# One issue order for a whole four-layer graph kernel, constants loaded on demand, a split layer norm, and an attention product built from rows times Wv·Wo

## The chip, the cores and the metric

The kernel runs on one core of a Trainium2 chip, in float32. A core has a matrix engine (TensorE, "PE" in the profile, with its weight loads shown apart as "PEld"), VectorE ("DVE"), ScalarE ("ACT"), GpSimd ("POOL") and SyncE ("SP", which here only issues transfers). Each engine works through its own list of instructions in order; between engines there are only semaphores. A transfer (DMA) is issued from an engine's queue, and an issue that must wait holds up what is behind it on that queue. Matrix products go to PSUM, of which there are 8 banks of 128 partitions by 512 float32.

The metric is the device time of one execution in microseconds (us).

## The reference

128 graphs of 64 nodes with 256 features, 8192 rows in all, go through four layers. Each layer computes `x = x + layer(relu(layernorm(x)))`:

```
# layer 0: two graph convolutions, then LSTMs over windows of 1, 2, 3 and 4 nodes
h = relu(adj @ (h @ Wg0 + bg0));  h = relu(adj @ (h @ Wg1 + bg1))
for p in 1..4:                       # LSTM p has its own weights
    wins = windows of p consecutive nodes of h
    h[last node of every window] = last hidden state of LSTM_p(wins)
# layer 1: normalised adjacency, two products, batch norm over all 8192 rows after each
h = relu(batchnorm((A_hat @ x) @ W1.T + b1));  out = batchnorm(h @ W2.T + b2)
# layer 2: diagonal, upper and lower part of adj, each with its own W
out = adj_0 @ (x @ W[0]) + adj_1 @ (x @ W[1]) + adj_2 @ (x @ W[2]) + bias
# layer 3: causal attention inside each graph, one head
q, k, v = split(x @ Wqkv);  y = softmax(q k^T / 16 + mask) @ v;  out = y @ Wo
```

The two batch norms need statistics over all rows, so nothing after them can begin for any row before all rows have passed.

## The kernel before, in words

The rows are cut into 16 blocks `s` of 512 rows (8 graphs), each 4 times 128 rows. Every stage runs over these blocks.

**Start (L86 to L118).** The identity and small constants are made, and thirteen loads of constants and first weights are issued from ScalarE's queue: the two adjacencies, bg0, Wg0, Wg1, bg1, the LSTM's and the batch norms' parameters, and W1 (L316, whose issue stands with them since a scheduler orders the work outside the hand-ordered parts). The blocks of x are loaded from SP's queue.

**Stage 1, `graph_part` (L265).** Five steps per block: layer norm and relu (`layernorm_relu`, L168: statistics on VectorE, the power −0.5 on GpSimd, the row scale and shift back on VectorE at L180, and four activations on ScalarE at L183), an aggregation over the adjacency (L193), the product with Wg0 (L289), a second aggregation, and the product with Wg1 (L300). `pipelined` (L220) issues in every round one step of each living block, the newest block first; a new block begins every `skew` rounds. The result `hT` stays in SBUF, features on partitions.

**Stage 2, the LSTMs (L357 to L556).** The order is written out by hand: `at(t, fn)` notes an action with a due time `t` in units of one gate product (a pair of a Wih and a Whh product, two instructions each of 512 columns), and the actions are issued in order of their due times. The gate products follow a Strassen-Winograd scheme with seven products in place of eight. `gate` (L417) has products on TensorE (L430, L436), copies out of PSUM on ScalarE and VectorE (L455), sums on VectorE (L452) and the activations on ScalarE (L448).

**Stage 3, `first_product` (L329).** Per block: x is loaded again on SP and the LSTM result copied on GpSimd (step 1); it is transposed back to rows and x added, the sum stored to DRAM (x1d), and the layer norm issued (step 2, L203, L183); it is aggregated with the normalised adjacency (step 3); multiplied by W1 (L348, step 4); and its batch-norm statistics are taken (step 5, L353). The first three blocks begin inside the LSTM's last step: `begin` and the `times` at L572 give the due times of their steps. The other 13 blocks follow with `pipelined`.

**Between (L582).** `bn_coeffs` turns the statistics of all four channel groups into scale and shift: aggregation, add, power on GpSimd, and three small operations.

**Stage 4, `second_product` (L629).** Eight pairs of blocks, again with due times: relu with scale and shift on ScalarE (L639), four sums T1 to T4 for each half k of the inner dimension (k=0 on VectorE, k=1 on GpSimd, L647 to L653), seven products (L663, each of two halves k), then sums and statistics. After it the weight products: Wq·Wk^T and Wv·Wo (L723, from transposes of Wqkv, L717).

**Stage 5, `rest` (L731).** Layers 2 and 3 per block, in ten steps with skew 2: load of x1d and scaling of y; transposes to rows, add, layer norm; three aggregations (L755); the product with the three W (L768), add, layer norm; transposes (L779); the qk product (L786, `h·Wq·Wk^T`); scores and softmax (L794 to L804); transposes of the exponentials (eT, L808); eT times h (yT, L816, copied out on ScalarE); and yT times Wv·Wo (L824), scaled by the softmax sums, added and stored. The order outside these hand-ordered parts (the constants' loads, `bn_coeffs`, the late weights) is left to a scheduler.

Of the kernel before, what the change touches and what calls it, by code (L numbers as in the profile page):

```python
# [9 lines left out]
F32 = mybir.dt.float32  # L10
AF = mybir.ActivationFunctionType
ALU = mybir.AluOpType
# [8 lines left out]
def kernel(ctx: ExitStack, tc: tile.TileContext, a: dict, out: bass.AP):  # L21
# [28 lines left out]

    const = ctx.enter_context(tc.tile_pool(name="const", bufs=1))
# [20 lines left out]
    def load_const(name, src, shape, pool=const):  # L72
        t = pool.tile(shape, F32, tag=name, name=name)
        nc.scalar.dma_start(t, src)
        return t

    def row_bcast(name, src, n, pool=const):
        t = pool.tile([P, n], F32, tag=name, name=name)
        nc.scalar.dma_start(t, bass.AP(tensor=src.tensor, offset=src.offset, ap=[[0, P], [1, n]]))
        return t  # L80

    def weight(name, src, pool=const):
        k, m = src.shape
        return load_const(name, src.rearrange("(c p) m -> p c m", p=P), [P, k // P, m], pool)
# [17 lines left out]
    bg0 = row_bcast("bg0", a["bg0"], D, first)  # L102
    wg0 = weight("wg0", a["Wg0"], first)
    wg1 = weight("wg1", a["Wg1"], first)
    bg1 = load_const("bg1", a["bg1"], [P, KC], first)
    bih = load_const("bih", a["bih"], [P, NL, NM])
    bhh = load_const("bhh", a["bhh"], [P, NL, NM])
    bn1 = load_const("bn1", a["bn1"], [P, 3, HC])
    bn2 = load_const("bn2", a["bn2"], [P, 3, KC])
# [18 lines left out]
    def adjacencies():  # L128

        nc.vector.tensor_add(lbias, bih, bhh)  # L130
# [37 lines left out]
    def layernorm_relu(pool, src, tag="ln_h", bufs=None, h=None):  # L168
# [4 lines left out]
        if h is None:  # L173
            h = pool.tile([P, Q, D], F32, tag=tag, name=tag, bufs=bufs)
        for q in range(Q):
# [5 lines left out]
                                       op0=ALU.mult, op1=ALU.mult)  # L181
        for q in range(Q):
            nc.scalar.activation(h[:, q, :], src[:, q, :], AF.Relu,  # L183
                                 bias=rn[:, 1, q : q + 1], scale=rn[:, 0, q : q + 1])
        return h
# [34 lines left out]
    def pipelined(gens, skew, live=()):  # L220

        gens, live, r = list(gens), list(live), 0
        with tc.manual_schedule():
            while gens or live:
                if gens and r % skew == 0:
                    live.insert(0, gens.pop(0))
                live = [g for g in live if next(g, "end") != "end"]
                r += 1  # L230
# [32 lines left out]
    with tc.tile_pool(name="pa", bufs=2) as pa, tc.tile_pool(name="pax", bufs=3) as pax:  # L263

        def graph_part(s):  # L265
# [3 lines left out]
            for q in range(Q if s == 0 else 1):  # L269
                part = slice(q, q + 1 if s == 0 else Q)  # L270
                nc.sync.dma_start(xt[:, part, :], x_r[s, :, part, :])
            h = layernorm_relu(pa, xt)
# [24 lines left out]
            for o in range(KC):  # L297
                p_ = bank()
                for c in range(KC):
                    nc.tensor.matmul(p_, wg1[:, c, ts(o, P)], g1[:, c, :],  # L300
# [3 lines left out]
                    t.rearrange("p (q n) -> p q n", q=Q), bcast_q(rs_row), bg1[:, o : o + 1],  # L304
# [11 lines left out]
    w1 = weight("w1", a["W1T"])  # L316
    pb, front = [], ExitStack()
# [11 lines left out]
    def first_product(s):  # L329
# [11 lines left out]
        h = layernorm_relu(lns, xt, h=hs.rearrange("p (q d) -> p q d", q=Q))  # L341
# [3 lines left out]
        for o in range(HC):  # L345
            p_ = bank()
            for c in range(KC):
                nc.tensor.matmul(p_, w1[:, c, ts(o, P)], ag[:, c, :],  # L348
                                 start=(c == 0), stop=(c == KC - 1))
            nc.scalar.activation(zslot(s, o), p_, AF.Identity, bias=bn1[:, 0, o : o + 1])  # L350
        yield
        for o in range(HC):
            nc.vector.bn_stats(st1[:, o, s, :], zslot(s, o))  # L353
        yield
# [204 lines left out]
    early = [None] * 3  # L559
# [12 lines left out]
    for s, times in enumerate(((10.5, 12.5, 25.5), (11.5, 28.5, 33), (13, 36))):  # L572
# [3 lines left out]
    with tc.manual_schedule():  # L576
        for _, _, fn, args in sorted(events, key=lambda e: e[:2]):
            fn(*args)
# [3 lines left out]
    def bn_coeffs(pool, stats, nch, prm, name):  # L582
# [289 lines left out]
```

## Time and profile before

| | us |
|---|---|
| median of 3 runs (1935.64 to 1936.22) | 1936.01 |
| the profiled execution's own time | 1937.42 |
| its span in the profile | 1935.7 |
| TensorE busy (98% of the span, 7060 matrix instructions) | 1890.1 |
| VectorE busy (57%) | 1099.9 |
| ScalarE busy (44%) | 852.1 |
| GpSimd busy (29%) | 557.4 |
| mean granted TensorE clock | 0.994 of full |

How to read the rows of the profile: in the list of waits, a row names the waiting engine, what it wrote and at which line, then what released it, and then the total time, the number of times and the longest, all in us. In a timeline a row has the start, the duration (of several alike instructions in a row, where `xN` stands at the end), engine, line, operation, output and inputs, sizes, and in brackets the idle time before it with what ended it. An engine with a `q` after its name is its instruction queue (issues of transfers). In the table by windows a row has the stretch and its length, then the busy time of TensorE, its weight loads, VectorE, ScalarE and GpSimd with the number of instructions, then the granted TensorE clock as a share of full speed, the share of the DMA engines and GB/s. In the chain a row has its start, its duration, engine and line, and the number of instructions. An x column of numbers like `128x512` gives partitions by elements.

### The profile page before, as it was taken

To read this page: it belongs to the slowest core of one execution; us is meant where nothing else is said; L and a number is where in the kernel's file an instruction comes from. 1 tells how busy PE (TensorE), PEld (TensorE's weight loads), DVE (VectorE), ACT (ScalarE), POOL (GpSimd) and SP (SyncE) were. 2 spreads that over 40 slices of the span, in tenths; PEclk is the share of its full clock that TensorE was granted. 3 is DMA by queue.
4 is the path that set the end of the run, shared out by engine and by line. 5 is a ranking of instruction groups with operands and counts; after the bars stand their busy time and mean duration, and the time that the engine had idled before them with its cause. 6 is when DMAs were issued, how large, how long until landed. Compare 5 with 4: busy or idle time off the path is not lost.

```text
span 1935.7 us, 19149 instructions
## 1 busy us (share of the span) xinstructions
PE 1890.1 (98%) x7060; PEld 1152.6 (60%) x7060; DVE 1099.9 (57%) x2132; ACT 852.1 (44%) x1430; POOL 557.4 (29%) x366
## 2 busy tenths in 40 slices
PE   7999999999999999999999999999899899999998
PEld 6776444444445666665444444555444688888887
DVE  6775777634546345445533334588686555556553
ACT  3554666534435335334433333344574343333332
POOL 1210322443325433232422224433153211111110
PEclk9999999999999999999999999999999999999999
DMA  5110000100001000000000001233100101111111
GB/s 157 55 34 1 1 1 13 31 0 0 0 0 44 1 1 1 1 1 22 0 0 1 1 0 55 88 109 109 41 0 22 33 11 34 44 44 45 44 34 44
DMA packets 49469, 54.29 MB, mean 28 GB/s; under 512 B 3040, under 2 KB 44768, under 8 KB 49376
## 3 DMA queue, kind: packets, MB, share of 16 engines
q1 hardware_dynamic: 45872, 49.81, 8.1%
q10 hardware_dynamic: 3504, 3.26, 0.5%
q8 instruction: 56, 0.92, 0.2%
q14 instruction: 37, 0.30, 0.1%
HBM read 36.28 MB, written 16.78 MB: 27 GB/s over the span
## 4 chain that ended last, share of the span: by engine, by line
PE 93%; DVE 2%; issue 2%; ACT 1%; POOL 1%; DMA 1%; DVEq 0%; POOLq 0%; ACTq 0%
PE ps L430 33%; PE ps L436 19%; PE ps L768 9%; PE ps L663 5%; PE ps L348 5%; PE ps L193 5%; PE ps L824 3%; PE ps L289 3%; PE ps L300 3%; PE ps L786 2%; PE ps L755 2%; PE ps L816 1%; PE ps L794 1%; PE ps L203 1%; PE ps L779 1%
## 5 line engine op out<-in xcount | busy, mean ns | idle before, releaser
L452 DVE TENSOR_TENSOR gate<-gate,ps 128x512 f32<-128x512 f32 (+2 forms) x378 | 223.7, 619 | 457.2 <-PE ps L436 377.7
L430 PE MATMUL ps<-tx,wih 128*128 128x512 f32 (+2 forms) x1008 | 449.4, 545 | 6.0 <-ACT gate L455 4.0
L430 PE MATMUL ps<-hT,wih 128*128 128x512 f32 (+2 forms) x756 | 338.5, 541 | 0.0
L430 PEld LDWEIGHTS ps<-tx,wih 128*128 128x128 f32 x1008 | 191.3, 191 | 196.9 <-issue 133.7
L455 ACT COPY gate<-ps 128x512 f32<-128x512 f32 (+2 forms) x252 | 134.5, 534 | 379.2 <-PE ps L436 325.5
L448 ACT ACTIVATE gate<-gate,lbias 128x512 f32<-128x512 f32 (+2 forms) x252 | 216.7, 860 | 153.9 <-DVE gate L452 153.9
L436 PE MATMUL ps<-h,whh 128*128 128x512 f32 (+2 forms) x576 | 257.5, 529 | 0.0
L430 PEld LDWEIGHTS ps<-hT,wih 128*128 128x128 f32 x756 | 143.7, 190 | 142.4 <-issue 80.2
L179 POOL TENSOR_TENSOR ln_rn<-ln_rn,mhalf 128x4 f32<-128x4 f32 x64 | 64.8, 1012 | 520.9 <-DVE ln_rn L178 520.9
L436 PE MATMUL ps<-th,whh 128*128 128x512 f32 (+2 forms) x432 | 193.4, 529 | 0.0
L436 PEld LDWEIGHTS ps<-h,whh 128*128 128x128 f32 x576 | 109.7, 191 | 100.8 <-issue 77.1
L768 PE MATMUL ps<-wl,ag 128*128 128x256 f32 x768 | 168.4, 379 | 0.0
L475 POOL TENSOR_TENSOR gate<-gate 128x1024 f32<-128x1024 f32 (+2 forms) x36 | 71.9, 2018 | 310.9 <-ACT gate L448 310.9
L768 PEld LDWEIGHTS ps<-wl,ag 128*128 128x128 f32 x768 | 144.7, 190 | 19.0
L183 ACT ACTIVATE ln_h<-x,ln_rn 128x256 f32<-128x256 f32 x128 | 66.4, 589 | 189.3 <-DVE ln_rn L180 189.3
L475 POOL TENSOR_TENSOR cell<-gate 128x1024 f32<-128x1024 f32 (+2 forms) x36 | 79.4, 2226 | 200.1 <-ACT gate L448 200.1
L436 PEld LDWEIGHTS ps<-th,whh 128*128 128x128 f32 x432 | 82.7, 191 | 76.3 <-issue 58.5
L348 PE MATMUL ps<-ag,w 128*128 128x512 f32 x256 | 112.3, 592 | 0.0
L475 POOL TENSOR_TENSOR cell<-gate,cell 128x1024 f32<-128x1024 f32 (+2 forms) x32 | 65.1, 2053 | 103.6 <-ACT gate L448 103.6
L455 DVE COPY gate<-ps 128x512 f32<-128x512 f32 (+2 forms) x126 | 78.6, 624 | 22.6 <-PE ps L436 22.6
L448 ACT ACTIVATE gate<-ps,lbias 128x512 f32<-128x512 f32 (+2 forms) x126 | 79.6, 632 | 4.0 <-PE ps L436 1.0
L480 ACT ACTIVATE gate<-cell 128x1024 f32<-128x1024 f32 (+2 forms) x72 | 68.1, 952 | 27.9 <-POOL cell L475 27.9
(187 smaller groups left out, 2587.6 us busy)
## 6 DMA issues: line engine op xcount, KB each, us to landing
xt<-in_x_dram SPq DMA_DIRECT2D x31, 512.0 KB, 4.4
x1d<-xt SPq DMA_DIRECT2D x16, 512.0 KB, 3.0
x<-x1d SPq DMA_DIRECT2D x16, 512.0 KB, 4.5
out_dram<-x SPq DMA_DIRECT2D x16, 512.0 KB, 3.2
wih<-in_WihT_dram SPq DMA_DIRECT2D x16, 256.0 KB, 4.9
whh<-in_WhhT_dram SPq DMA_DIRECT2D x12, 256.0 KB, 5.0
wqkv<-in_Wqkv_dram ACTq DMA_DIRECT2D x1, 768.0 KB, 4.3
wl<-in_W_dram ACTq DMA_DIRECT2D x3, 256.0 KB, 3.1
```

Source lines behind the costliest of these rows:

```text
L183: nc.scalar.activation(h[:, q, :], src[:, q, :], AF.Relu, bias=rn[:, 1, q : q + 1], scale=rn[:, 0, q : q + 1])
L193: nc.tensor.matmul(p_[:, ts(q, P)], h[:, q, ts(c, P)], mT, start=True, stop=True)
L348: nc.tensor.matmul(p_, w1[:, c, ts(o, P)], ag[:, c, :], start=(c == 0), stop=(c == KC - 1))
L430: nc.tensor.matmul(wide(p_[:, :N]), wih[0][:, OF[k], gi, :], x_, start=first_, stop=(j == 0), skip_group_check=True)
L436: nc.tensor.matmul(p_[:, :N], whh[0][:, OF[k], gi, :], h_, start=False, stop=True, skip_group_check=True)
L448: nc.scalar.activation(to, r[bank_][:, :N] if bank_ else to, fn, bias=lbias[:, l, m : m + 1])
L452: nc.vector.tensor_add(slot(n, hc), slot(n, hc), r[bank_][:, :N])
L455: op(slot(n, hc), r[bank_][:, :N])
L475: fn(*((t["G"] if isinstance(t, dict) and "G" in t else st["c"])[:, n, :, : st["N"]] for t in tiles))
L480: nc.scalar.activation(o_, c, AF.Tanh)
L663: nc.tensor.matmul(banks[name], w2[:, OF[j], k, :], x_, start=(new and k == 0), stop=(k == 1), skip_group_check=True)
L768: nc.tensor.matmul(p_[:, q, :], ag[:, c, k, ts(q2 + q, P)], wl2[k][:, c, :], start=(n == 0), stop=(n == 3 * KC - 1))
```

## The change

All of the kernel is now issued in the order in which it is written; no part is left to a scheduler.

- **Constants on demand.** ScalarE's queue keeps the two adjacencies, bg0 and Wg0. Wg1, bg1, the LSTM biases, the batch-norm parameters and W1 are loaded from SP's queue, in front of block 3's x. A small Relu activation (`warm`) stands on ScalarE behind the loads. The late weights (the three W, bias, Wqkv, Wo) go to SP's queue too, behind the last store of stage 3.
- **Layer norm in two parts.** `layernorm_relu` becomes `norm_of` (statistics and row scale) and `normalize_relu` (the four activations). In `first_product`, for blocks 0 to 2, there is a step between the two, and the due times are new.
- **Batch-norm coefficients by halves.** In the last block, `bn_coeffs` is called after every second channel group.
- **First pair of the second product.** Of the eight relus two run on VectorE (two operations each), the sums of k=1 run on VectorE in place of GpSimd, and the first two products are issued as halves k=0, k=1. The order of the first relus changes.
- **Wv·Wo** is formed after block 0's transposes in `rest`.
- **Attention.** In place of `(eT·h)·(Wv·Wo)`, `hw = h·(Wv·Wo)` is formed beside qk, in the same step, and the output is `eT·hw`. One step per block goes away; `ln_h3` has two buffers in place of four.

```diff
+    ctx.enter_context(tc.manual_schedule())
...
-    wg1 = weight("wg1", a["Wg1"], first)
...
+    bg0 = row_bcast("bg0", a["bg0"], D, first, nc.scalar)
+    wg0 = weight("wg0", a["Wg0"], first, nc.scalar)
+    warm = const.tile([P, 1], F32, tag="warm", name="warm")
+    nc.scalar.activation(warm, mhalf[:, 0:1], AF.Relu)
+    con = {}
+
+    def more_constants():
+        con["wg1"] = weight("wg1", a["Wg1"], first)
+        con["bg1"] = load_const("bg1", a["bg1"], [P, KC], first)
+        con["bih"] = load_const("bih", a["bih"], [P, NL, NM])
+        con["bhh"] = load_const("bhh", a["bhh"], [P, NL, NM])
+        con["bn1"] = load_const("bn1", a["bn1"], [P, 3, HC])
+        con["bn2"] = load_const("bn2", a["bn2"], [P, 3, KC])
+        con["w1"] = weight("w1", a["W1T"])
...
+            if s == 2:
+                more_constants()
             h = layernorm_relu(pa, xt)
...
-        h = layernorm_relu(lns, xt, h=hs.rearrange("p (q d) -> p q d", q=Q))
+        rn = norm_of(lns, xt)
+        if s < len(early):
+            yield
+        h = hs.rearrange("p (q d) -> p q d", q=Q)
+        normalize_relu(h, xt, rn)
...
         for o in range(HC):
             nc.vector.bn_stats(st1[:, o, s, :], zslot(s, o))
+            if s == NS - 1 and o % 2:
+                bn_coeffs(lns, co1, st1, o - 1, o + 1, con["bn1"], "bn1")
...
-    for s, times in enumerate(((10.5, 12.5, 25.5), (11.5, 28.5, 33), (13, 36))):
+    for s, times in enumerate(((10.5, 12.5, 16.5, 28.3), (11.5, 22.3, 26.2, 31), (13, 33, 36.5))):
...
             def relu(n, c):
-                nc.scalar.activation(z(n, c), z(n, c), AF.Relu, bias=co1[:, 1, c : c + 1],
-                                     scale=co1[:, 0, c : c + 1])
+                if i == 0 and n == 1 and c % 2 == 0:
+                    nc.vector.tensor_scalar(z(n, c), z(n, c), co1[:, 0, c : c + 1],
+                                            co1[:, 1, c : c + 1], op0=ALU.mult, op1=ALU.add)
+                    nc.vector.tensor_scalar_max(z(n, c), z(n, c), 0.0)
...
-            for k, (n, c) in enumerate(((0, 1), (0, 3), (0, 0), (0, 2), (1, 0), (1, 2), (1, 1), (1, 3))):
+            for k, (n, c) in enumerate(((0, 1), (0, 0), (0, 3), (0, 2), (1, 0), (1, 2), (1, 1), (1, 3))):
                 at((-6.3, -5.8, -5.3, -4.4, -3.9, -3.4, -2.4, -1.9)[k], relu, n, c)
-            for k, engine in enumerate((nc.vector, nc.gpsimd)):
+            for k, engine in enumerate((nc.vector, nc.gpsimd if i else nc.vector)):
...
-                at(t, product, name, j)
-            at(2, lambda: evict(y(0, 0), 0, "a"))
+                if i == 0 and t < 2:
+                    at(t, product, name, j, (0,))
+                    at(t + 1.1, product, name, j, (1,))
+                else:
+                    at(t, product, name, j)
+            at(2.2, lambda: evict(y(0, 0), 0, "a"))
...
             to_token_major(lambda c, q: y[c][:, ts(q, P)], x1, x2)
+            if s == 0:
+                weight_product(2, wo, wvo)
...
-            h = layernorm_relu(pc, x3, "ln_h3", 4)
+            h = layernorm_relu(pc, x3, "ln_h3")
...
                 nc.scalar.copy(qk[:, o, :], p_)
+            hw = pc.tile([P, Q, D], F32, tag="hw", name="hw")
+            for q2 in range(0, Q, 2):
+                p_ = bank().rearrange("p (q d) -> p q d", q=2)
+                for q in range(2):
+                    for c in range(KC):
+                        nc.tensor.matmul(p_[:, q, :], h3T[:, c, ts(q2 + q, P)], wvo[:, c, :],
+                                         start=(c == 0), stop=(c == KC - 1))
+                nc.scalar.copy(hw[:, q2 : q2 + 2, :], p_)
...
-            yT = pc1.tile([P, KC, SUP], F32, tag="yT", name="yT")
-            for c in range(KC):
-                p_ = bank()
-                for q in range(Q):
-                    nc.tensor.matmul(p_[:, ts(q, P)], h[:, q, ts(c, P)], eT[:, ts(q, P)],
-                                     start=True, stop=True)
-                nc.scalar.copy(yT[:, c, :], p_)
             yield
             for q2 in range(0, Q, 2):
                 p_ = bank().rearrange("p (q d) -> p q d", q=2)
                 for q in range(2):
-                    for c in range(KC):
-                        nc.tensor.matmul(p_[:, q, :], yT[:, c, ts(q2 + q, P)], wvo[:, c, :],
-                                         start=(c == 0), stop=(c == KC - 1))
+                    nc.tensor.matmul(p_[:, q, :], eT[:, ts(q2 + q, P)], hw[:, q2 + q, :],
+                                     start=True, stop=True)
```

The rest of the diff puts `bn_coeffs` on a range of channel groups with a given output tile, gives the load helpers a queue argument (SP where none is named), wraps a weight product into the function `weight_product`, and moves the reciprocal of the softmax sums behind the copy of eT.

## The prediction

> **What bounds the kernel now.** I read the page first (busy shares, the 40 slices, the chain by engine), then the waits of TensorE, then the timeline round every wait over 1 us. The page:
>
> ```profile
> PE 1890.1 (98%) x7060; PEld 1152.6 (60%) x7060; DVE 1099.9 (57%) x2132; ACT 852.1 (44%) x1430; POOL 557.4 (29%) x366
> ...
> PE   7999999999999999999999999999899899999998
> ...
> PE 93%; DVE 2%; issue 2%; ACT 1%; POOL 1%; DMA 1%; DVEq 0%; POOLq 0%; ACTq 0%
> ```
>
> TensorE is 98% busy and 93% of the chain; four slices of 40 fall below 9. To be won is TensorE work that goes away, or time in which it stands or runs slowly. Where it stands (total us, times, longest):
>
> ```profile
> PE ps L193 <- ACT ln_h L183: 8.2, 1, 8.2
> ...
> PE ps L755 <- ACT ln_h L183: 5.2, 1, 5.2
> PE ps L663 <- ACT hS L639: 4.9, 1, 4.9
> PE ps L430 <- ACT gate L455: 4.0, 3, 3.0
> PE ps L193 <- ACT hs L183: 3.9, 1, 3.9
> ...
> PE ps L755 <- ACT qk L788: 1.6, 2, 1.0
> ```
>
> All are at seams between stages. TensorE's timeline puts them in place:
>
> ```profile
> 14.95 6.70 PE L193 MATMUL ps<-adjT_bd,ln_h 128*128 128x128 f32 x32 [8.18 <-ACT ln_h L183]
> ...
> 1202.39 2.08 PE L430 MATMUL ps<-tx,wih 128*128 128x512 f32 x2 [2.96 <-ACT gate L455]
> ...
> 1236.37 3.98 PE L193 MATMUL ps<-ahT,hs 128*128 128x128 f32 x16 [3.95 <-ACT hs L183]
> ...
> 1395.32 2.07 PE L663 MATMUL ps<-hS,w 128*128 128x512 f32 x2 [4.86 <-ACT hS L639]
> ...
> 1505.73 4.45 PE L755 MATMUL ps<-adj,ln_h 64*128 64x192 f32 x32 [5.20 <-ACT ln_h L183]
> ```
>
> After each wait the matmuls are slow: 16 aggregation matmuls take 3.98 us here and 1.95 at 1222.73, a pair 2.08 instead of 1.02. The windows give the granted clock (third column from the end): 0.50 after the wait, 1.00 again some 7 us later. A wait so costs itself and about 3 us more.
>
> ```profile
> 1202.00:1203.00 1.00, 0.61 (x1) 0.50 (x2) 0.00 (x0) 1.00 (x2) 0.00 (x0) 0.50 0.01 3
> 1209.00:1210.00 1.00, 1.00 (x4) 0.52 (x3) 0.69 (x1) 0.00 (x0) 0.00 (x0) 1.00 0.00 0
> ```
>
> **The change part by part**, against the profiled execution (1937.42 us, span 1935.7), which lies 1.41 above the median of 1936.01.
>
> *Start.* ScalarE's queue issues 13 loads before its first activation; the row scale of block 0 is ready long before:
>
> ```profile
> 8.38 0.16 DVE L180 SCALAR_TENSOR_TENSOR ln_rn<-ln_mv,ln_rn 128x4 f32<-128x4 f32 x1 [1.21 <-POOL ln_rn L179]
> ...
> 13.00 1.28 ACT L183 ACT_TABLE_LOAD   x1 [13.00 <-DMA wih<-in_WihT_dram]
> ```
>
> Six loads of constants and W1's leave this queue, and the table load follows the wg0 issue (this and wg1's end at 6.55): it ends by 7.8, and block 0 is normalised from 8.6 (first quarter 0.6) instead of 14.3. The first aggregation starts at 9.2, not 14.95, a gain of 5.7 for block 0. Block 1's row scale still comes at 13.57, so its aggregation waits to 14.2, and TensorE, idle between, stays at half clock. By then block 0's Wg0 product has moved ahead of block 2's aggregation: with block 1's aggregation (32 half-clock matmuls took 6.5, so 3.3) to 17.5 and the product (3.5 at full clock, more where cold), block 2's aggregation starts at about 22.0 where it was 24.94. I take 3.0; bounds 0 (all eaten by the cold clock) and 5.7. The seven loads go to SP in front of block 3's x: it was issued at 16.40, waiting for its buffer, which now comes free near 11; the seven issues cost 0.45 each (the last W1 issue took 0.45) and land within 5.2, so by 16 to 17, against a need near 22. Cover 5 us. One layer's Wih, loaded at 9.06 before, is now loaded after stage 1, some 60 us ahead of its weight sums. Both cost nothing.
>
> *Stage 1 and the LSTM.* Every engine's instructions stand in the same order as before until the last LSTM step: no change, the gain at the start is carried through.
>
> *The LSTM's end.* ScalarE stood 10.05 us behind the row scale (L180, ready at 1199.7) of the normalise it had been given too early, so the gate copy L455 came late, and TensorE waited for its bank. At 1236.37 block 1's aggregation waited in the same way. Now the row scale is asked for one event earlier than the normalise: block 0's transposes at 12.5 and its normalise at 16.5, 4 units of 1.715 us (two pairs of 0.86) = 6.9 us, where the chain from transposes to scale took 1193.25 to 1199.7 = 6.5; block 1 has 3.9 units (6.7 us) and its aggregation 8.2 us later, for four activations of 2.08. Removed: standing 1199.28 to 1202.39 (3.1) and 1232.26 to 1236.37 (4.1); slow clock 1202.39 to 1209.00 = 6.61 for work of 3.43 (3.2), and 1236.37 to 1243.16 = 6.79 for 3.51 (3.3). Sum 13.7. What comes late next: a bank freed by VectorE 0.9 us before it is needed, one by ScalarE 1.0 us, block 3's copies on POOL 1.4 us, block 3's x (on SP behind block 2's store and four W2 loads) 1.6 us, by adding the rows' durations in the new order. If one fails, TensorE stands a little; if by 3 us, it also goes slow. Bounds 8 and 13.7.
>
> *First to second product.* The coefficients are now made in two halves: those of channels 0 and 1 hang on the second statistics (1388.5) and come at about 1391.5; those of 2 and 3 (eight small operations and POOL's 1.01) at 1395.8, where all came at 1394.42. The first two half products (k=0) start at 1392.4, not 1395.32, then k=1 waits to about 1396.6: idle of 1.9 and 2.6 instead of 4.86. VectorE gets two relus (two operations each, about 0.5) and POOL's four sums for pair 0; the eight sums take 0.69 each alone (0.69 at 1398.12; 1.16 to 1.76 where POOL worked beside it), 1397.8 to 1403.3, no later than before. The sixth product then ends at 1401.9 if the clock stays, 1404.3 if not; before at 1404.66. I take 1.2; bounds 0 and 2.7. The six late loads go from ScalarE to SP behind the last store, a hundred us before their use at 1494: nothing.
>
> *Second product to the rest.* The Wv·Wo product (1.73) moves behind block 0's transposes, into the idle 5.20: transposes start at 1498.9 (scaled y is ready then) instead of 1499.49, so the wait ends 0.6 earlier, and 3.5 idle are left. If that idle no longer cools the clock, 4.45 falls to 2.87, 1.6 more. I take 1.0; bounds 0.5 and 2.3.
>
> *The rest.* Per round the chain has these, of 25.96 us:
>
> ```profile
> 1599.06 1.79 PE ps L816 x16
> ...
> 1615.95 3.46 PE ps L824 x16
> ```
>
> They become 16 matmuls of 256 columns (hw, 3.46) and 8 (out, 1.73): 0.06 a round, 1.0 in 16. ScalarE copies two hw banks instead of two yT banks, the same 0.57 each; the reciprocal stays on VectorE beside TensorE's work, and fewer ln_h3 buffers suffice since `h` is read only by the transposes: nothing. In the first rounds hw fills the place where L755 waited for the qk copies (1546.33 to 1547.35, 1545.69 to 1546.15, 1568.21 to 1569.37: 2.6). I take 2.6; bounds 1 and 3.1 (all of the waits there). In steady rounds the nearest copy is 0.9 us ahead of its need. The tail only sees work that was done earlier: 0.
>
> Sum: 3.0 + 13.7 + 1.2 + 1.0 + 1.0 + 2.6 = 22.5. 1937.42 − 22.5 = 1914.9 for a profiled execution, 1913.5 as a median. All lower ends: 0+8+0+0.5+0+1 = 9.5, so 1926.5; all upper ends: 5.7+13.7+2.7+2.3+1.0+3.1 = 28.5, so 1907.5.
>
> A rule weighed: the trace cooled the clock in a wait of 2.96 us at 1202.39 and did not in one of 3.22 us at 1527.6 (transposes there 0.175 each, 1.40 for eight). [...]
>
> **Rivals.**
> - *The cover at the LSTM's end is too thin.* One of the four slacks of 0.9 to 1.6 us fails and a wait of about 3 us with a slow clock comes back: 6.3 less, 1919.8. For: SP's queue is longer there. Against: four separate slacks must each be misjudged by their whole size.
> - *The clock eats the start.* TensorE stays at half clock until after block 2's aggregation as before: 3.0 less, and with both gaps cold at the second product (0.8 less) 1917.3. For: half clock until 21.4 before. Against: block 0's product comes earlier by order alone.
> - *Slower: ScalarE falls behind in the rest.* Its queue now has qk's two copies, hw's two copies and the exps closer together; if hw's banks come free late, every round waits. 22.5 + 3.9 is reached at 1.65 us a round of 16, that is copies 2.5 us later than by the 0.9 of slack; price at that point 1940. For: L755 waited 1.0 for the qk copies in two early rounds. Against: ScalarE is 44% busy and in the steady rounds waited for nothing.
> - *It does not do what it says.* If the LSTM's end kept its waits, 13.7 less: 1927.2. Against: the events are spelled out, and the new order has the split.
>
> **How the numbers follow.** About 0.2% (3.9 us) tells from no change here. Forecast 0.66, thin cover 0.13, clock 0.13, ScalarE behind 0.04, no effect 0.04. Faster by over 0.2%: 0.94; within: 0.02; slower: 0.04. The range takes in the first two rivals and most of the bounds: 1907 to 1924.
>
> **What would show it.** First aggregation at about 9.2 and the LSTM's first matmul some 3 us earlier; no wait over 1 us and no 0.50 clock between 1190 and 1245; block 0's W1 product starting about 13.7 + 3.0 earlier than 1244.03; two short waits in place of 4.86 at the second product; L755's wait near 3.5; rounds of 25.9. It is wrong if the LSTM's end has a wait over 2 us, if a round exceeds 26.2, or if TensorE waits for a load.

## The result, and the profile after

The changed kernel takes 1918.22 us in the median of four runs (1916.92 to 1918.94) where the kernel before took 1935.83 beside it: 17.6 us less, a ratio of 0.9909 (95% interval 0.9892 to 0.9926). The forecast was 1913.5 with a range of 1907 to 1924. The direction and the range hold; the time is 4.7 us above the forecast, and 4.9 us of the 22.5 are missing. Run a second time beside the last experiments, it took 1917.25 (1916.66 to 1918.94) against 1936.04.

The profiled execution has a span of 1917.0 us against 1935.7, so 18.7 less. TensorE is busy 1884.5 us. First the waits of TensorE in the changed kernel (total us, times, longest):

```profile
PE ps L207 <- ACT ln_h L191: 6.7, 2, 3.7
PE ps L132 <- DMA adjT_bd<-in_adjT_dram: 4.2, 1, 4.2
PE ps L783 <- ACT ln_h L191: 3.5, 1, 3.5
PE ps L807 <- DVE ag L788: 3.2, 1, 3.2
PE ps L684 <- ACT z L660: 1.6, 1, 1.6
PE ps L684 <- ACT hS L660: 1.5, 1, 1.5
...
PE ps L684 <- ACT hS L688: 1.1, 1, 1.1
...
PE ps L217 <- DVE hS L762: 0.9, 1, 0.9
PE ps L851 <- DVE eT L845: 0.8, 1, 0.8
```

Both waits at the LSTM's end are gone, and so are the qk copies. The wait before the second product (4.9) is now two of 1.5 and 1.6, and a third of 1.1 follows among its first products, for the copy at L688 out of a bank, which the prediction did not list. The wait that stood before the rest is 3.5 instead of 5.2. Two more lines are new: the transposes at L217 wait 0.9 for the scaled y, and the last product 0.8 for the copy of eT. L807 waits 3.2 as before.

TensorE's timeline of the changed kernel at the places of the prediction:

```profile
8.02 3.70 PE L207 MATMUL ps<-adjT_bd,ln_h 128*128 128x128 f32 x16 [3.03 <-ACT ln_h L191]
15.38 3.98 PE L207 MATMUL ps<-adjT_bd,ln_h 128*128 128x128 f32 x16 [3.67 <-ACT ln_h L191]
...
23.79 1.95 PE L207 MATMUL ps<-adjT_bd,ln_h 128*128 128x128 f32 x16
...
1229.04 7.03 PE L365 MATMUL ps<-ag,w 128*128 128x512 f32 x16
...
1376.95 1.98 PE L684 MATMUL ps<-hS,w 128*128 128x512 f32 x4 [1.48 <-ACT hS L660]
1380.58 1.98 PE L684 MATMUL ps<-z,w 128*128 128x512 f32 x4 [1.65 <-ACT z L660]
...
1487.87 4.99 PE L783 MATMUL ps<-adj,ln_h 64*128 64x192 f32 x32 [3.47 <-ACT ln_h L191]
...
1510.27 1.97 PE L807 MATMUL ps<-ident,ln_h 128*128 128x128 f32 x8 [3.22 <-DVE ag L788]
...
1908.72 3.45 PE L851 MATMUL ps<-hw,eT 128*128 128x256 f32 x8 [0.78 <-DVE eT L845]
```

Compared with the rows of before: block 0's first aggregation starts at 8.02 instead of 14.95, but block 1's only at 15.38. Block 0's W1 product starts at 1229.04 instead of 1244.03. The four matmuls at 1376.95 take 1.98, full speed (the same took 2.07 for two before). L783 takes 4.99 for what is 2.87 at full speed, L807 1.97 where before it took 1.40, and the last L851 3.45 where the others take 1.89. Windows of the changed kernel show why, by the granted clock (third column from the end):

```profile
1490.00:1491.00 1.00, 1.00 (x10) 1.00 (x8) 0.56 (x1) 0.48 (x1) 1.00 (x1) 0.50 0.00 0
...
1511.00:1512.00 1.00, 1.00 (x6) 1.00 (x6) 1.00 (x3) 1.00 (x4) 0.00 (x0) 0.50 0.00 0
...
1910.00:1911.00 1.00, 1.00 (x4) 0.82 (x3) 0.50 (x2) 0.00 (x0) 0.00 (x0) 0.50 0.00 0
```

TensorE is at work there, at half clock (0.50). A ledger by stage, from the starts of the same instructions in both traces (the stretch before minus the stretch after):

| stretch | before | after | gained | forecast |
|---|---|---|---|---|
| start to block 0's transposes in the LSTM | 1193.25 | 1191.94 | 1.3 | 3.0 |
| to block 0's W1 product | 50.78 | 37.10 | 13.7 | 13.7 |
| to the first transpose of Wqkv | 250.00 | 247.43 | 2.6 | 1.2 |
| to the first product with the three W | 17.01 | 17.25 | −0.2 | 1.0 |
| to the second such product | 18.66 | 19.73 | −1.1 | 0 |
| to the end | 406.00 | 403.55 | 2.4 | 3.6 |
| span | 1935.7 | 1917.0 | 18.7 | 22.5 |

So 13.7 of 18.7 us come from the LSTM's end, exactly as worked out; the shortfall stands at the start, at the seam before the rest, and in the rest. The experiments ask for each why.

### The profile page after: what moved, and what is told of

Read it like the earlier page. It is cut to its first block, busy times and chain, and to the rows that moved or that the text cites. A ratio compares the mean times of both kernels' runs of the same rounds, so it can differ in the third digit from the quotient of the medians.

```text
span 1917.0 us, 18932 instructions
## 1 busy us (share of the span) xinstructions
PE 1884.5 (98%) x6932; PEld 1148.2 (60%) x6932; DVE 1098.9 (57%) x2144; ACT 849.0 (44%) x1429; POOL 552.0 (29%) x363
## 4 chain that ended last, share of the span: by engine, by line
PE 95%; DVE 2%; POOL 1%; ACT 1%; issue 1%; DMA 0%; ACTq 0%; DVEq 0%; POOLq 0%
PE ps L449 33%; PE ps L455 19%; PE ps L796 9%; PE ps L365 6%; PE ps L684 5%; PE ps L207 4%; PE ps L303 3%; PE ps L822 3%; PE ps L314 3%; PE ps L814 3%; PE ps L783 2%; PE ps L830 1%; PE ps L217 1%; PE ps L851 1%; PE ps L807 1%
```

## The experiments

Unless said otherwise each edit is to the changed kernel. Stretches and starts are from the profiled execution of each; medians are of four runs. The runs were made in sets, and the kernel before ran beside each: it took 1935.83 beside the changed kernel, 1936.62 beside bg0 first, the LSTM's end alone, all undone before the second product and the attention product as before, 1937.42 beside the two fillings and the two halves of the second product's seam, and 1936.04 beside the last three. So medians of different sets can be compared to about 1.5 us, no closer.

**bg0 first.** In the changed kernel VectorE waits 2.98 us for bg0 at the row sums:

```profile
10.52 0.35 DVE L130 TENSOR_SCALAR rsb<-bg,rs_col 128x256 f32<-128x256 f32 x1 [2.98 <-DMA bg<-in_bg_dram]
```

The load was issued at 0.81 before, first on its queue though written behind the adjacencies, and is issued at 3.63 now, in the order as written; it lands after 6.8 us instead of 4.1. Block 1's statistics stand behind it in VectorE's order.

```diff
+    bg0 = row_bcast("bg0", a["bg0"], D, first, nc.scalar)
     adjT_bd = block_diag("adjT_bd", a["adjT"])
     adj_bd = block_diag("adj_bd", a["adj"])
-    bg0 = row_bcast("bg0", a["bg0"], D, first, nc.scalar)
```

> The changed kernel, with the load of bg0 issued first on ScalarE's queue instead of behind the four adjacency loads. Theory A (bg0 is what VectorE waits for: in the changed kernel it stands 2.98 us at the row-sum product until bg0 lands at 10.5, and block 1's layer norm is queued behind it): that wait goes, block 1's row scale comes at 12 to 13.4 instead of 14.7, its aggregation starts at 12.7 to 14.1 instead of 15.38, and everything after is 1.0 to 2.7 us earlier: 1915.5 to 1917.2 against 1918.2. Theory B (the half clock of the first matmuls sets the start, not the load): block 2's aggregation stays within 0.5 us of 23.79, the time within 0.5 of 1918.2.

Measured: 1914.43 (1913.51 to 1916.91). The timeline of this kernel, VectorE and TensorE:

```profile
8.95 0.35 DVE L130 TENSOR_SCALAR rsb<-bg,rs_col 128x256 f32<-128x256 f32 x1
...
12.96 0.16 DVE L185 SCALAR_TENSOR_TENSOR ln_rn<-ln_mv,ln_rn 128x4 f32<-128x4 f32 x1 [1.12 <-POOL ln_rn L184]
```
```profile
13.81 3.87 PE L207 MATMUL ps<-adjT_bd,ln_h 128*128 128x128 f32 x16 [0.94 <-ACT ln_h L191]
...
20.97 1.95 PE L207 MATMUL ps<-adjT_bd,ln_h 128*128 128x128 f32 x16
```

The wait for bg0 is gone and block 1's row scale comes 1.6 us earlier than in the changed kernel (13.12 against 14.69). Block 2's aggregation starts at 20.97 instead of 23.79, block 0's transposes in the LSTM at 1189.11. Theory A holds for the wait and for block 1; the median lies below its range, and not all of the 2.8 belongs to bg0: eight profiled executions with the start of the changed kernel have these transposes at 1189.7 to 1191.9, mean 1190.4. The two executions with only bg0 moved at the start have 1189.1 and 1189.6 (the second is the last kernel below), so bg0 first brings 0.8 to 1.3, and the start as changed has gained 2.8 (1.3 in the worst, which is the one profiled first).

The rest of the 2.8 is the clock. The trace's own record of the granted clock has no entry for the first microseconds; the views show 1.00 there, while the matmuls run at half rate (block 1's 16 take 3.87 to 3.98 us in the five executions below, block 2's 1.95 at full clock). The last entry of the start is the one from which the clock is full until the later seams:

| execution | block 1's aggregation starts | clock full from | block 2's aggregation starts |
|---|---|---|---|
| changed kernel | 15.38 | 21.53 | 23.79 |
| changed kernel again | 15.14 | 19.65 | 22.73 |
| filled waits | 14.33 | 20.58 | 22.79 |
| halves undone | 14.24 | 18.05 | 21.49 |
| bg0 first | 13.81 | 17.44 | 20.97 |

In each of the five, block 2's aggregation starts 5.34 us (within 0.01) behind the mean of the two times before it, as it must if the work between runs at half rate until the clock is full (the changed kernel's clock was full from 11.29 to 14.70 too, while TensorE mostly stood). So in these five half of every delay, of block 1 or of the clock, arrives at block 2. Of the 2.8 between the changed kernel and bg0 first, block 1's earlier start makes 0.8 and the clock's earlier rise 2.0. The filled waits and the halves undone have the same edits at the start and block 1 within 0.1; the clock parts them by 1.3. Three further executions fit the relation within 0.02; the run with all undone and the one with the VectorE work undone (both below) had full clock until 16 us and come 0.1 to 0.2 earlier than by it.

**The LSTM's end alone**, put into the kernel before: the split of the layer norm and the due times, nothing else.

```diff
-        h = layernorm_relu(lns, xt, h=hs.rearrange("p (q d) -> p q d", q=Q))
+        rn = norm_of(lns, xt)
+        if s < 3:
+            yield
+        h = hs.rearrange("p (q d) -> p q d", q=Q)
+        normalize_relu(h, xt, rn)
...
-    for s, times in enumerate(((10.5, 12.5, 25.5), (11.5, 28.5, 33), (13, 36))):
+    for s, times in enumerate(((10.5, 12.5, 16.5, 28.3), (11.5, 22.3, 26.2, 31), (13, 33, 36.5))):
```

> The kernel before, with only the layer norm of blocks 0 to 2 split and the new due times at the LSTM's end. Theory A (each part acts on its own seam and the gains add): 13.7 us less than before, 1922.1 from 1935.8, with block 0's W1 product at 1230.3 instead of 1244.03 and no wait over 1 us between 1190 and 1245. Theory B (the LSTM's end also needs the other order of loads: late weights on SP, W1 early): less than 11 us, with a wait left at the LSTM's end.

Measured: 1927.0 (1926.65 to 1927.17), 9.6 us less than the kernel before. Theory A gave 13.7, theory B less than 11 with a wait left; neither is right. The timeline of TensorE in this kernel:

```profile
1229.99 2.31 PE L358 MATMUL ps<-ag,w 128*128 128x512 f32 x5
...
1492.48 4.95 PE L765 MATMUL ps<-adj,ln_h 64*128 64x192 f32 x32 [5.20 <-ACT ln_h L184]
...
1514.84 1.97 PE L789 MATMUL ps<-ident,ln_h 128*128 128x128 f32 x8 [3.22 <-DVE ag L770]
1516.60 1.91 PE L209 MATMUL ps<-ident,hS 128*128 128x128 f32 x8
1518.31 11.68 PE L778 MATMUL ps<-wl,ag 128*128 128x256 f32 x48
```

The stretch to the W1 product is 37.10 where it was 50.78: the whole 13.7, with no wait left. The rest of it is given back where nothing was edited. The wait of 3.22 at 1511.6 is the one that the kernel before has too; there the transposes behind it took 1.40 and 1.04, here 1.97 and 1.91, and the product behind them 11.68 instead of 10.53. In all: 0.8 more up to the transposes of Wqkv, 0.5 at L765, 1.4 and 1.2 behind L789, together 3.8 of 13.7 + 0.4. The same waits cost more, because the clock falls or stays by the moment at which a wait begins (behind the one of 3.22 it is 0.50 from 1513.82 to 1520.65 here, and 1.00 throughout in the kernel before). What that moment counts against is shown below.

**The seam before the second product as before** (coefficients at once, all relus on ScalarE, the k=1 sums on GpSimd, whole products, and the old order of the first relus), and then each half of this undone alone. The coefficients come after all four statistics here, so the wait is 6.1, not 4.9.

```diff
-            if s == NS - 1 and o % 2:
-                bn_coeffs(lns, co1, st1, o - 1, o + 1, con["bn1"], "bn1")
+        if s == NS - 1:
+            bn_coeffs(lns, co1, st1, 0, HC, con["bn1"], "bn1")
...
-                if i == 0 and n == 1 and c % 2 == 0:
+                if False:
...
-            for k, engine in enumerate((nc.vector, nc.gpsimd if i else nc.vector)):
+            for k, engine in enumerate((nc.vector, nc.gpsimd)):
...
-                if i == 0 and t < 2:
+                if False:
```

> The changed kernel, with the seam between first and second product as before: all coefficients at once, all relus on ScalarE, the k=1 sums of pair 0 on GpSimd, the first products whole. Theory A (the two short waits keep the clock at full, where one wait of 4.9 us halves it): 2.6 us slower than the changed kernel, 1920.8, a wait of about 4.9 us and the granted clock at 0.50 after it. [...]

The halves undone, the work left on VectorE (the first and last hunk above, and the old order of the first relus):

> The changed kernel with the coefficients made at once and the first products whole again, but with two relus and all sums of pair 0 still on VectorE. Theory A (splitting the one long wait in two is what keeps the clock at full): 3 us slower than the changed kernel in the stretch from block 0's W1 product to the end of the second product, with a wait of 5 to 6 us and 0.50 clock. Theory B (the work on VectorE brings it): less than 1 us slower there.

The halves kept, the work put back on ScalarE and GpSimd (the two middle hunks):

> The changed kernel with the halves kept, but all relus of pair 0 on ScalarE and its k=1 sums on GpSimd. Theory A (the halves alone bring the gain): within 1 us of the changed kernel in the stretch from block 0's W1 product to the end of the second product, no 0.50 clock there. Theory B: 1.5 to 3 us slower there, since the relus come late and sums on GpSimd and VectorE slow each other (1.16 to 1.76 us a sum against 0.69).

| | halves | VectorE work | W1 product to transposes of Wqkv | 0.50 clock there | median |
|---|---|---|---|---|---|
| all undone | no | no | 251.30 | 6.8 us | 1921.49 |
| halves undone | no | yes | 250.77 | 6.8 us | 1918.84 |
| VectorE work undone | yes | no | 248.84 | none | 1916.92 |
| changed kernel | yes | yes | 247.43 | none | 1918.22, 1917.25 |

The wait that decides, in the kernel with all undone, and in the one with halves (VectorE work undone):

```profile
PE ps L684 <- ACT hS L660: 6.1, 1, 6.1
```
```profile
PE ps L684 <- ACT z L660: 1.7, 1, 1.7
PE ps L684 <- ACT hS L688: 1.6, 1, 1.6
PE ps L684 <- ACT hS L660: 1.5, 1, 1.5
```

In the stretch itself theory A holds for the halves: they bring 2.5 to 3.3 us, the VectorE work 0.5 to 1.4. With all undone the stretch is 3.9 longer where theory A gave 2.6, as the wait is 6.1; with the VectorE work undone it is 1.4 longer, outside theory A's 1 us and short of theory B's 1.5. All four executions with one long wait here (4.85 to 6.1, before and the LSTM's end alone among them) lose the clock, none of the nine with short waits does. The medians do not show it cleanly: the kernel with the VectorE work undone has the lower median although its stretch is 1.4 longer.

**The attention product as before**, with yT and one step more:

```diff
-            hw = pc.tile([P, Q, D], F32, tag="hw", name="hw")
-            ...
+            yT = pc1.tile([P, KC, SUP], F32, tag="yT", name="yT")
+            ...
-                    nc.tensor.matmul(p_[:, q, :], eT[:, ts(q2 + q, P)], hw[:, q2 + q, :],
-                                     start=True, stop=True)
+                    for c in range(KC):
+                        nc.tensor.matmul(p_[:, q, :], yT[:, c, ts(q2 + q, P)], wvo[:, c, :],
+                                         start=(c == 0), stop=(c == KC - 1))
```

> The changed kernel, with the attention product as before: yT from eT and h, then yT times Wv Wo, one step more per block, four ln_h3 buffers. Theory A (the rest won 2.5 us: 1.0 of work and 2.6 of waits on the qk copies, less 1.1 lost in a tail with a halved clock): 2.5 us slower, 1920.7, with waits of L755's kind on the qk copies back in the third and fourth round (2.6 in sum). Theory B (the waits come only from the phase of the rounds, and the new order has none by chance): about 1.0 slower, 1919.2, and no such waits.

Measured: 1918.84 (1917.35 to 1920.93), so only 0.6 to 1.6 slower than the changed kernel, where theory A gave 2.5; the kernel before took 0.6 to 0.8 more beside it too, so the medians do not tell the two apart. The waits on the qk copies are back, as theory A said:

```profile
PE ps L783 <- ACT qk L816: 1.7, 2, 1.0
```

From the second product with the three W to the end it has 406.0 us, as the kernel before, against 403.55: 2.5 by stage. The median hides part of it: in this profiled execution the clock did not fall before L807, in the changed kernel's it did (1.1). The stage is worth more at equal clock. With the filled waits and in the last kernel below, the clock is full from the second such product to the last matmul, as it is here and in the kernel before: there the stretch takes 402.08, 3.9 less than 406.0.

**Filled waits.** Products that nothing reads, into a bank that nothing reads: three of 512 columns before the rest's first L783, three before its first L807, one of 256 on either side of the last transposes of the exponentials.

```diff
+    def fill(n, left, right, cols=P):
+        p_ = bank()
+        for _ in range(n):
+            nc.tensor.matmul(p_[:, :cols], left, right, start=True, stop=True)
...
                 weight_product(2, wo, wvo)
+                fill(3, ident, wqkv[:, 0, :512], 512)
...
+            if s == 0:
+                fill(3, ident, wqkv[:, 0, :512], 512)
             h3T = pc.tile([P, KC, SUP], F32, tag="h3T", name="h3T")
...
+            if s == NS - 1:
+                fill(1, ident, wqkv[:, 0, :256], 256)
             p_ = bank()
...
+            if s == NS - 1:
+                fill(1, ident, wqkv[:, 0, :256], 256)
             eT = pc1.tile([P, SUP], F32, tag="eT", name="eT")
```

> The changed kernel, with TensorE kept at work by products that nothing reads: three of 512 columns (0.86 us each) in the wait of 3.5 us before the rest's first L783, three in the wait of 3.2 us before its first L807, and one of 256 columns (0.43) on either side of the last exponentials' transposes. They lie inside waits and move nothing. Theory A (what the later seams lost is the halved clock): no 0.50 clock after 1470 us, the stretch from the start of L783 to the end of the following transposes 3.7 us instead of 5.9, L807 1.1 instead of 2.0, the last L851 1.9 instead of 3.5; 3 to 5 us faster than the changed kernel, 1913.5 to 1915, and runs closer together. Theory B (the seams lost to late data): the same starts, no more than 0.5 us faster.

Measured: 1916.52 (1915.67 to 1917.47), 1.7 us less than the changed kernel's first median and short of theory A's 3 to 5. Its timeline:

```profile
1483.24 2.74 PE L131 MATMUL ps<-wqkv,ident 128*128 128x512 f32 x6
1486.88 3.37 PE L790 MATMUL ps<-adj,ln_h 64*128 64x192 f32 x32 [0.90 <-ACT ln_h L197]
...
1507.56 4.31 PE L131 MATMUL ps<-wqkv,ident 128*128 128x512 f32 x6 [3.13 <-DVE ag L795]
...
1908.95 1.99 PE L864 MATMUL ps<-hw,eT 128*128 128x256 f32 x8 [0.35 <-DVE eT L858]
```

Two of three work: the aggregations take 3.37 instead of 4.99, the last product 1.99 instead of 3.45. The third was my mistake: the filling itself needs a bank, waits 3.13 for the same copy as L807, and then runs in front of it at the clock that has fallen; from the first to the second product with the three W it costs 22.57 instead of 19.73. It shows that this wait ends with a freed bank.

**Fillings at the start** together with bg0 first: nine 128-column products before the row sums, five behind, eight behind block 0's aggregation.

> The changed kernel with bg0 loaded first (as in the run with bg0 first) and with 128-column products that nothing reads at the start: nine before the row sums, five behind them and eight behind block 0's aggregation. Theory A (the first matmuls run at half rate because TensorE had stood): block 0's and block 1's aggregations take 1.9 us instead of 3.9, block 2's aggregation starts at 18.5 to 20 instead of 20.97, 1 to 2.5 us faster than with bg0 first alone at equal seams later. Theory B (the layer norm of block 2, on VectorE, sets the start by then): no more than 0.5 us earlier.

Measured: 1915.15 (1913.82 to 1915.98), no faster than bg0 first (1914.43), block 2's aggregation at 20.54 instead of 20.97. Theory B holds: with TensorE kept at work the aggregations are paced by the layer norm, four activations in 2.08 us, and take 2.86. The clock is recorded as full from 6.24 here. Block 1's aggregation is at 14.39, 0.6 later than with bg0 first alone, as its row scale came later; from there to block 2's it is 6.15 us instead of 7.16. So an early full clock is worth 1.0 in this stretch even against the earliest rise in the table above.

**Wv·Wo in front of the transposes again:**

```diff
         weight_product(0, wT[:, KC : 2 * KC, :], wqk)
+        weight_product(2, wo, wvo)
...
-            if s == 0:
-                weight_product(2, wo, wvo)
```

> The changed kernel with the Wv Wo product in front of block 0's transposes again. Theory A (the move gains only 0.3 us, because the transposes then wait 0.85 us for the scaled y on VectorE): 0.3 us more from the first transpose of Wqkv to the first L783 (11.7 against 11.4), a wait of about 5.2 us before L783, no difference in time that can be told. Theory B (the product inside the wait keeps TensorE busier and the clock up): 1 us or more slower there.

Measured: 1915.79 (1915.27 to 1918.47). The stretch from the transposes of Wqkv to L783 is 11.70 against 11.40, as theory A has it. The wait is 5.2 instead of 3.5, and L783 loses the clock either way (4.55 here, 4.99 and 4.71 in two executions of the changed kernel).

**The changed kernel again, and the parts that paid put together:** bg0 first, the fillings before L783 and at the last transposes.

> The changed kernel once more, as the measure for the two runs beside it. Theory A (what differs between its executions is the start, 1189.7 to 1191.9 at block 0's transposes in the LSTM in six profiles of the same start, and where the 3.41 us grid of the clock falls on the later seams): a spread of 2 to 4 us among runs and a median of 1916 to 1918.5, that is 18.5 to 21 under the kernel before. Theory B (the first profile is typical): 1918 to 1919, spread under 1 us.

> The changed kernel with bg0 loaded first, with three products of 512 columns that nothing reads in the wait before the rest's first L783, and with one of 256 columns on either side of the last exponentials' transposes; none in front of L807. Theory A (bg0 gives 1.3 at the start, the fillings take 1.2 and 1.4 of slow clock away, and the parts add): 3 to 5 us faster than the changed kernel on the same chip, 1912 to 1914. Theory B (the gains were phases of the grid, which shift with the start): within 1.5 us of the changed kernel.

Measured on one chip: 1917.25 (1916.66 to 1918.94) and 1913.92 (1913.55 to 1914.59), so 3.3 us faster than the changed kernel. Its timeline:

```profile
1485.52 3.37 PE L790 MATMUL ps<-adj,ln_h 64*128 64x192 f32 x32 [0.90 <-ACT ln_h L197]
...
1506.31 1.97 PE L814 MATMUL ps<-ident,ln_h 128*128 128x128 f32 x8 [3.23 <-DVE ag L795]
```

Theory A's range holds. The seam before L783 and the tail are at full clock; L814 (L807 of the changed kernel) lost it in this execution, 1.4. Against bg0 first alone (1914.43, ranges overlap) no gain can be told in the medians. Of the changed kernel's repetition theory A holds: its runs spread over 2.3 us, and its second profile starts 1.1 us earlier than the first, loses 2.5 instead of 1.1 behind L807 and nothing in the tail.

**What the moment counts against.** Read in windows of 0.1 us, the changes of the granted clock of one execution all lie on one grid of 3.4133 us: in the changed kernel the first and the last, at 14.70 and 1915.92, are 557 such steps apart. In the kernel before they are at 1201.8, 1208.6, 1235.9, 1242.7, 1392.9, 1399.7, 1505.6 and 1509.0; the remainders by 3.4133 are 0.25 to 0.33. In the changed kernel nine changes from 14.7 to 1915.9 have remainders of 1.02 to 1.11, in the others the remainder is another one for each (0.1 with the filled waits, 2.5 with all undone before the second product, 1.7 with the LSTM's end alone). So where the grid lies differs from execution to execution.

The wait before L807 is 3.2 us long in all twelve executions that have it unfilled; in five the clock fell, in seven it stayed. What parts them is where the wait begins: 0.2, 0.7, 1.1, 1.2 and 1.3 us behind a point of that execution's grid where it fell, 1.4, 1.5, 1.6 and 1.7 to 1.9 (four times) where it stayed. So the clock fell where TensorE stood for 2.1 us or more of one stretch of the grid, and stayed at 2.0 or less.

The wait before L783 of 3.5 or 5.2 cost the clock in all eleven, the waits of 1.5 to 1.7 before the second product in none of nine. Both fit the same count. Take, for every wait of more than 1 us from 1190 us on in the thirteen executions, the largest part of it that lies in one stretch: the smallest with which the clock fell is 2.02 (before L783 in the changed kernel), the largest with which it stayed is 1.98 (before L807 with the halves undone).

Of the eight unfilled tails with the new attention product, six lost it. In these six all the time that TensorE stands round the last transposes (1.3 us, and the four transposes themselves are drawn out to 1.49 from 0.60) lies in one stretch; in the two that kept the clock, the repetition of the changed kernel and the one with all undone, a point of the grid divides it (0.4 and 0.9, 0.5 and 0.8).

## Why the prediction was right or wrong

- **LSTM's end, 13.7.** Right to 0.1, in all executions with the new times (37.10 or 37.11). The cover that the first rival doubted held every time; no wait is left there. The argument against that rival was weaker than it sounds: one slack that failed would have been enough, not all four.
- **Start, 3.0.** Right in the mean (2.8 over eight profiles), 1.3 in the one compared. There the step "Block 1's row scale still comes at 13.57" fails: it comes at 14.69, since bg0's load stands four issues later in ScalarE's queue and the row sums wait for it in front of block 1's statistics on VectorE. I counted the loads that leave the queue, and not the order of those that stay (block 0's own aggregation came at 8.02, before the 9.2 of the sum, since its row scale was ready earlier). In five other kernels with this start VectorE's wait for bg0 ended earlier (at 9.28 to 9.49 instead of 10.52) and the row scale came at 13.5 to 13.9, near the step. The larger part is the step "the product (3.5 at full clock, more where cold)": block 0's product takes 4.80, as the clock is full only from 21.53, and block 1's aggregation at half clock takes 3.8 to the product's start, not the 3.3 read from a row whose end already ran at full clock (before, the record has full clock from 20.76). Of the 1.8 us by which block 2's aggregation misses the 22.0 of the sum, block 1's later start makes 0.6 and the clock, by the relation in the table, 1.2. So the rival that the clock eats the start was right in part: its condition, half clock until after block 2's aggregation, is not met (that one takes 1.95), but the clock takes most of what is missing here.
- **First to second product, 1.2 of 0 to 2.7.** The mechanism was right (two waits, 1.5 and 1.6 instead of 1.9 and 2.6, the sums on VectorE), apart from the third wait of 1.1 behind them, and the size too small: 2.6. The term mis-sized is the value taken between warm (2.7) and cold (0.4); none of nine executions with short waits went cold.
- **Second product to the rest, 1.0.** Wrong: −0.2. The step "transposes start at 1498.9 (scaled y is ready then)" gave 0.6; they wait 0.85 for the second half of y, and 0.3 is what the move gains (run with Wv·Wo in front). L783 then takes 4.99 instead of 4.45, which loses 0.5 again. And the clock, of whose 1.6 the 1.0 counted a quarter as saved, fell in all eleven unfilled executions, with the wait at 3.5 as at 5.2; in the changed kernel's first profile only just, with 2.02 us of the stretch idle.
- **The rest, 3.6.** 2.4 measured, 3.9 at equal clock (402.08 against 406.0), so the work and the waits were sized nearly rightly and the difference is the clock. The waits on the qk copies go (2.6) and the round is 25.90 instead of 25.96. The step "The tail only sees work that was done earlier: 0" failed: with less work beside the last softmax the clock falls before the last product in six of eight, by where the grid lies, 1.4 in the profiled one. With the fillings it stays in both executions that have them, as in the two unfilled ones that kept it (352.4 against 353.9 us from the fourth product with the three W to the end).
- **A wait costed at nothing.** L807's 3.2 us were there before at full clock; I left them out as unchanged. In the profiled execution they cost 1.1 more, by the grid alone.
- **The slower rival**, ScalarE behind in the rest: not seen, the rounds are 25.90 and wait for nothing.
- **A sign of being wrong that did show.** TensorE does wait for a load: its first matmuls, the row sums (L132), wait 4.2 us for adjT's. It cost nothing, since the first aggregation waits for ScalarE until 8.02 in any case.
- **The length of a wait.** The prediction set a wait of 2.96 us that cooled the clock beside one of 3.22 that did not. The experiments bear out that the length alone does not decide: the waits of 1.5 to 1.7 before the second product kept the clock in all nine executions, 3.2 before L807 lost it in five of twelve, 3.5 or 5.2 before L783 in all eleven. Of the waits of more than 1 us from 1190 us on, those lost the clock in which TensorE stood for 2.02 us or more of one grid stretch of 3.41, and those kept it in which it stood for 1.98 or less.

What stays open: what sets the point from which the clock is full at the start (17.4 to 21.5 us without fillings there), why VectorE's wait for bg0 ends 1.0 to 1.2 us later in the changed kernel's first profile (10.52) than in the five other kernels with this start (9.28 to 9.49), and why the four runs of the LSTM's end alone agree within 0.5 us when the changed kernel's spread over 2.

## What to carry to other kernels

Where the clock falls, a wait of the bounding engine at a seam has two prices, itself and the slow clock after it (3.1 and 3.2 us at 1202.39 in the kernel before); splitting one wait into two short ones (1.5 and 1.6 in place of 4.9), or filling it with a product whose operands and bank are there (the aggregations behind it take 3.37 in place of 4.99), removed the second here. When an edit shortens an early stage, all later waits fall elsewhere on the clock's grid, so untouched seams change too, in either sign (3.8 us lost with the LSTM's end alone; from the first to the second profile of the changed kernel 1.4 lost behind L807, and the tail's 1.4 won): compare by stage, and put several executions beside each other before a us or two is given a cause. When loads leave a queue, look at the order of those that remain, and at what is queued behind the first instruction that waits for one of them.

## What the runs showed of the hardware

- All changes of the granted clock of an execution lie on a grid of 3.4133 us, and where it lies differs from execution to execution (remainders from 0.1 to 2.8). A wait of 3.2 us lost the clock in five of twelve executions, at a price of 1.1 to 2.6 us, and it was the place of its beginning on the grid that decided: 1.3 us behind a point or less it fell, at 1.4 or more it stayed.
- At the start the views show a granted clock of 1.00 in the kernel before and with bg0 first, while the aggregation matmuls run at about half rate (32 in 6.70 us before; 16 later take 1.95). The trace's clock record is empty there: its first entry is full clock at 20.76 in the kernel before and at 17.44 with bg0 first, where the 16 matmuls at 13.81 take 3.87 and the product at 17.52 runs at full rate (3.62). An empty record is not a full clock.
- The same load of 128 KB landed 4.1 us after its issue at 0.81 in the kernel before, and 6.8 us after its issue at 3.63 in the changed kernel. What it shared the way with was not tested.
- Sixteen aggregation matmuls that follow the layer norm directly take 2.86 us with TensorE warm: they are paced by the four activations in front of them (2.08), not by TensorE.
